# Down's weight folds spread over places, one fetch moved ahead of the transposing loads, and the fold steps of gate and up shifted

## The chip, the cores and the metric

The kernel runs on one core of one Trainium2 chip. A core has five engines with a queue each, which run in order and wait for each other only through semaphores: TensorE (PE in the profile, its weight loads are PEld), VectorE (DVE), ScalarE (ACT), GpSimd (POOL) and SyncE (SP). SP computes nothing; it issues the transfers between DRAM and the on-chip memories, which 16 DMA engines then carry out. TensorE writes its results to PSUM, a small memory that VectorE and ScalarE read. The metric is the device time of one execution in microseconds; before the change the median of three runs was 1569.95 us (1569.58 to 1570.46).

## The reference

The input x is (8, 512, 512) in float32: 8 sequences of 512 tokens and 512 channels. Cut to what matters:

```python
xn = layernorm(x)                                   # over channels
q, k, v = xn @ Wq.T + bq, xn @ Wk.T + bk, xn @ Wv.T + bv
kv = cumsum((elu(k) + 1) * v, axis=tokens)          # linear attention, elementwise per channel
s = ((elu(q) + 1) * kv * 32**-0.5) @ Wo.T + bo
h = fwht(xn * SU_ug) / 64                           # normalized Hadamard transform over 512
u = (h @ W_up.T) * (Wscale_ug[:2048] * 64)
g = (h @ W_gate.T) * (Wscale_ug[2048:] * 64)
d = fwht(silu(g) * u * SU_dp) / 64                  # over 2048
d = (d @ W_down.T) * (Wscale_dp * 64)
out = x + s * silu(d)
```

## The kernel before

**Products.** Every matrix product is done with seven products instead of eight for each 2 x 2 split of its operands. Both operands carry seven factors, at the indices P1 to P7: four are given, the other three (and a changed P7) are sums and differences of them ("encode"). The seven products are summed in PSUM and by VectorE. The helper group (L442) does it for q, k, v, gate and up with 512 tokens in the columns; token_groups (L512) for o and down, with tokens in the rows; hidden_unit with block_product (L622, L803) does it on two levels at once for gate and up together ("gu"). TensorE works in float32.

**Pairs.** The outer loop takes the eight sequences in four pairs p. A pair runs k, v, q twice (attention), then four units u of gate, up and their gated product "ho", with o after the first unit and half of down after the second and the fourth. In the first pair the weights have to be made first: gate and up in units 0 to 2 come from raw weights, one matrix block at a time, and only unit 3 and all units of the later pairs take ready two-level weights ("gu", streamed from d_gu).

**Folded weights.** The Hadamard transforms and the signs are moved into the weights. For one block of gate or up, folded_w (L919) loads the raw block and returns three steps with a number of places each: butterflies (four VectorE additions), fold (two TensorE products with the 128 x 128 Hadamard matrix `had`, evicted by four ScalarE activations, L945) and encode (four VectorE operations, L305 to L308). For a block f of 4 or more, encode also queues inner_w, which forms the two-level factors (L408) and stores them to d_gu.

**Down's weights** are made during the first pair. begin_down (L1144) and chain_down (L1149) take the matrix in four blocks o of 128 columns, 1 MB each: load_down (L960) loads block o into the working tile rd; butterflies_down (L963) queues ten VectorE operations of 128 x 1024 (two scales, L974, and four levels of two, L969); fold_down (L983) issues four TensorE products with `had`, each evicted by four ScalarE activations (L994), and stores the block to wd_f in DRAM. Once all four are there, first_half_down (L999) loads what the first half of down needs, forms its factors and stores them to d_down 0; the second half is made in four parts by down_w (L374), queued behind groups 16 to 19. wd_made counts the stored parts of each half; a half is ready at 4.

**Places.** The order of the work around these is written by hand. `at(n, fn)` (L422) enters a step n places ahead in an agenda; advance runs the agenda. A group takes 14 places, and a place is half of the time of a product over two blocks (two 128 x 512 matmuls each). VectorE work that is not urgent goes into a list with later() and is popped by pace() (L89) behind an output on VectorE, up to a given time of work (1.7 us by default in group); `urgent` goes ahead of `idle`. catch_up (L96) pops all of it. block_product doesn't pace.

**Weights ahead.** `queue` (L1067) holds all weights in the order of their use, ask(n) (L1082) requests them so that n are ahead (three), and get_w takes one. The steps of a requested block are entered at `e["place"] = max(now + steps[k][0], place + 4)` (L1105): the butterflies of the block two ahead, the fold and the encode of the next one. For a weight of down, stream_w (L323) first makes sure that its half is ready: it pops the lists until wd_made is 4 (L330 to L333).

**The hand-over to the next pair.** After the last unit, next_tokens (L238) loads the normalized tokens of the next pair transposed ("z", eight loads of 256 KB from d_x, squares, L225) and queues VectorE's transposes. Then the first half's result of down, d, is fetched back from DRAM (fetch, L748, two of 1 MB), later s and y, and down's second half begins. z of the odd sequence, d, s, y and the tiles a, v, u, r of a unit share six buffers, t8; the streamed weights share four, wpool.

**From program order to queues.** The framework plans the queue of each engine from the traced program with its own costs: an instruction can be issued ahead of one that was traced before it if its inputs and its buffer are ready sooner by those costs. keep_in_program_order (L938, L987) holds a fold behind what was traced before it on TensorE, issue_after holds paced work behind its output, and background (L75) lowers the priority of what it traces.

Of the kernel before, what the change touches and what calls it, by code (L numbers as in the profile page):

```python
# [8 lines left out]
F32 = mybir.dt.float32  # L9
# [12 lines left out]
def kernel(  # L22
# [66 lines left out]
    def pace(ins, us):  # L89
        while us > 0 and (urgent or idle):  # L90
            t, fn, args = (urgent or idle).pop(0)
            with tc.issue_after(ins.ins):
                fn(*args)
            us -= t
# [228 lines left out]
    def stream_w(name):  # L323
        w = new_w("%s_%s" % (name[0], name[1] if type(name[1]) is int else "%d_%d" % name[1]))
        if name[0] == "gu":
            u, i = name[1]
            nc.sync.dma_start(w, inner[u][:, i])
        elif name[0] == "down":
            h, i = name[1]
            while wd_made[h] < 4:  # L330
                assert urgent or idle
                _, fn, args = (urgent or idle).pop(0)
                fn(*args)  # L333
            w = by_factor(w, 4)
            nc.sync.dma_start(w, wd[h][:, i])
        else:
            nc.sync.dma_start(flat(w), kept["%s_%d" % name])
            if name[0] == "o":
                w = by_factor(w)
        return w  # L340
# [98 lines left out]
        return ps.tile([P, n, L // n], F32, tag=tag, bufs={"px": 3, "py": 1, "pz": 2, "t": 2}[tag], name=f"{tag}_{name}")  # L439


    def group(name, ws, rhs, dst, then, bias=(None, None)):  # L442

        n = len(ws)
        u = n

        def product(p, i, first):
            for k in range(n):  # L450
                r = rhs(k, i)
                nc.tensor.matmul(  # L452
                    p.rearrange("p a t -> p (a t)") if len(r.shape) == 2 else p, ws[k][:, i, :], r,
                    start=(first and k == 0), stop=(k == n - 1), skip_group_check=True,
                )

        def snapshot(what, i):
            s = snap.tile([P, L], F32, tag="s", name=f"{what}_{name}")
            b = bias[min(i, 1)]
            p = px.rearrange("p a t -> p (a t)")  # L460
            if b is None:
                nc.scalar.copy(s, p)
            else:
                nc.scalar.activation(s, p, AF.Identity, bias=b)
            return s

        def output(i, s, p):
            pace(nc.vector.tensor_tensor(dst[i], s, p.rearrange("p a t -> p (a t)"), ALU.add), 1.7)  # L468

        px, py, pz = (bank(t, name, 2) for t in ("px", "py", "pz"))  # L470
        sums = {}

        def p1():
            product(px, P1, True)
            sums["a"] = snapshot("sa", 0)

        def p2():
            product(py, P2, True)
            output(0, sums["a"], py)

        def p6():
            product(px, P6, False)
            sums["b"] = snapshot("sb", 1)

        def p7():
            product(pz, P7, True)

        def p5():
            product(px, P5, False)
            sums["c"] = snapshot("sc", 2)  # L490
            output(2, sums["c"], pz)

        def p3():
            product(px, P3, False)

        def p4():
            product(pz, P4, False)
            output(1, sums["b"], pz)
            then(px.rearrange("p a t -> p (a t)"))

        at(0, p1)
        at(u, p2)
        at(3 * u, p6)
        at(5 * u, p7)
        at(6 * u, p5)
        at(9 * u, p3)
        at(11 * u, p4)
        advance(7 * u)
        between()
# [174 lines left out]
    def attention(p, xo, co, get_w):  # L684
        def project(m, g, then):
            w = get_w(m, g)
            r = t8.tile([P, 2, 2, L], F32, tag="t", name=f"{m}_{p}_{g}")
            b = (col("b" + m, g), col("b" + m, g + 2))

            def whole(px):  # L690
                nc.scalar.activation(r[:, 0, 1], px, AF.Identity, bias=b[0])  # L691
                then(r)

            group(
                f"{m}_{p}_{g}", [w[:, 0], w[:, 1]], x_rhs(xo),
                (r[:, 0, 0], r[:, 1, 0], r[:, 1, 1]), whole, b,
            )

        def elu_plus_one(r, name):
            neg = t8.tile([P, 2, 2, L], F32, tag="t", name=f"neg_{name}")  # L700
            for h in range(2):
                nc.scalar.activation(neg[:, h], r[:, h], AF.Relu, scale=-1.0)
                nc.scalar.activation(neg[:, h], neg[:, h], AF.Exp, scale=-1.0)
                nc.vector.scalar_tensor_tensor(r[:, h], r[:, h], 1.0, neg[:, h], ALU.add, ALU.max)

        def heads(g):
            phi = {}

            def with_k(k):
                phi["k"] = k  # L710
                elu_plus_one(k, f"k_{p}_{g}")

            def with_v(v):
                k = phi["k"]
                for h in range(2):
                    nc.gpsimd.tensor_tensor(v[:, h], v[:, h], k[:, h], ALU.mult)  # L716
                at(4, lambda: sums(k, v))

            def sums(k, v):
                for h in range(2):  # L720
                    for s in range(2):
                        nc.vector.tensor_tensor_scan(  # L722
                            k[:, h, s], ones.to_broadcast([P, L]), v[:, h, s], 0.0, ALU.mult, ALU.add
                        )

            def with_q(q):
                k = phi["k"]
                elu_plus_one(q, f"q_{p}_{g}")
                for h in range(2):
                    nc.vector.scalar_tensor_tensor(  # L730
                        co[:, g, h : h + 3 : 2, :], k[:, h], QSCALE, q[:, h], ALU.mult, ALU.mult
                    )
                encode_tokens(nc.gpsimd, co[:, g])

            project("k", g, with_k)
            project("v", g, with_v)
            project("q", g, with_q)

        for g in range(2):
            heads(g)  # L740
# [178 lines left out]
    def folded_w(name, src, f, room=None):  # L919
# [32 lines left out]
                with background():  # L952
                    inner_w(name, f - NU, folded[name, f - NU], w)

        return w, [(6, butterflies), (5, fold), (9, encode)]

    folded = {}
    wd_f = dram.tile([FF, D], F32, tag="wd_f", name="wd_f")

    def load_down(o):  # L960
        nc.sync.dma_start(rs[:, o % 2], wdown_t[:, o * P : (o + 1) * P].rearrange("(c p) e -> p c e", p=P))

    def butterflies_down(o, then):  # L963
# [16 lines left out]
                later(1.2, half, i, dst, src, h)  # L980
        later(0.0, then)

    def fold_down(o):  # L983
        r = rs[:, o % 2]
        for a in range(NF // 4):
            p = ps.tile([P, 4, P], F32, tag="t", name=f"pwd_{o}_{a}")
            tc.keep_in_program_order(  # L987
                nc.tensor.matmul(
                    p.rearrange("p c e -> p (c e)"), had,
                    r[:, 4 * a : 4 * a + 4].rearrange("p c e -> p (c e)"), start=True, stop=True,  # L990
                )
            )
            for c in range(4):
                nc.scalar.activation(  # L994
                    r[:, 4 * a + c], p[:, c], AF.Copy, scale=su_dp[:, 4 * a + c : 4 * a + c + 1]
                )
        nc.sync.dma_start(wd_f[:, o * P : (o + 1) * P].rearrange("(c p) e -> p c e", p=P), r)

    def first_half_down():  # L999

# [80 lines left out]

    def ask(n):  # L1082
        while queue and len(ahead) < n:
            p, m, g = queue.pop(0)
            w, steps = (first_w if p == 0 and m not in ("down", "gu") else later_w)(m, g)
            ahead.append({"key": (m, g), "w": w, "steps": steps, "traced": 0, "asked": 0, "place": 0})

# [56 lines left out]
    def begin_down():  # L1144
        nc.sync.dma_start(wsc_r, wscale_dp.partition_broadcast(P))
        load_down(0)
        at(12, lambda: chain_down(0))

    def chain_down(o):  # L1149
        def folded_block():  # L1150
            fold_down(o)
            if o + 2 < KD:
                at(8, lambda: load_down(o + 2))
            if o + 1 == KD:
                at(8, first_half_down)

        def then():
            at(10, folded_block)
            if o + 1 < KD:
                at(4, lambda: chain_down(o + 1))  # L1160

        butterflies_down(o, then)
# [14 lines left out]
    for p in range(B // 2):  # L1177
# [11 lines left out]
        for u in range(NU):  # L1189
# [23 lines left out]
            if u == 1:  # L1213
                if p == 0:
                    weights_ahead(NU - 1)
                down(p, 0, hos, get_w)
                if p == 0:
                    inner_tokens(xo)
                hos = []
        if more:  # L1220
            catch_up()
            next_tokens(2 * p + 2, xo)
        ds = [fetch(f"d_{p}_{s}") for s in range(2)]
        ss, ys = [], []
        at(7, lambda: ss.extend([fetch(f"s_{p}_{s}") for s in range(2)]))
        at(15, lambda: ys.extend([load_y(p, s) for s in range(2)]))
# [52 lines left out]
```

## Time and profile before

| | us |
|---|---|
| median of three runs | 1569.95 |
| profiled execution | 1564.62 |
| its span | 1562.80 |
| TensorE busy | 1529.4 |
| VectorE busy | 985.1 |
| GpSimd busy | 497.5 |
| ScalarE busy | 418.8 |

The profile shows one execution. "Busy" counts the time in which an engine computes; a queue that only waits or issues transfers is not busy. A wait is told as the engine and its line, the engine and line that released it, and the sum, number and longest of such waits; a timeline line as start, length, engine, line, operation, output <- inputs, shapes and number, with the idle time before it in brackets. A name such as px_gate is the PSUM tile px of the product gate, pw and pwd are the PSUM tiles of the folds of gate or up and of down, w_down is a weight tile of down and d_down the DRAM tensor it comes from.

### The profile page before, as it was taken

How to read it: one execution, taken by the hardware profiler on the slowest of the kernel's cores; microseconds unless marked ns; L12 is line 12 of the kernel's file. 1: busy time of each engine (PE TensorE's matmuls, PEld its weight loads, DVE VectorE, ACT ScalarE, POOL GpSimd, SP SyncE). 2: the span in 40 equal slices, each digit the busy share in tenths (PEclk: the TensorE clock that was granted, in tenths of full speed). 3: DMA queues.
4: the chain of work that ended last, by engine and by line, in shares of the span. 5: the costliest groups of instructions: out<-in, count | busy, mean ns of one | idle time of the engine just before them, and what ended most of it. 6: DMA issues, size and time to landing. Idle time of an engine off the chain costs nothing.

```text
span 1562.8 us, 15732 instructions
## 1 busy us (share of the span) xinstructions
PE 1529.4 (98%) x5924; PEld 1127.0 (72%) x5924; DVE 985.1 (63%) x1379; ACT 418.8 (27%) x664; POOL 497.5 (32%) x280
## 2 busy tenths in 40 slices
PE   7999999998999999999999999999999999999998
PEld 3335545845884588888885488888886468888887
DVE  5897785677866674716676574725675476543673
ACT  4443341142114521112215431111212431111211
POOL 4633144004321262304612235301622236110731
PEclk9999999999999999999999999999999999999999
DMA  8244867797785344344575434336474233535462
GB/s 280 78 153 152 268 218 225 232 275 270 200 304 196 91 158 155 108 152 165 157 286 213 102 137 148 135 102 195 153 249 171 85 106 117 185 99 177 155 260 85
DMA packets 197693, 273.31 MB, mean 175 GB/s; under 512 B 56817, under 2 KB 155121, under 8 KB 193393
## 3 DMA queue, kind: packets, MB, share of 16 engines
q1 hardware_dynamic: 197472, 272.27, 53.3%
q8 instruction: 47, 0.77, 0.2%
q14 instruction: 30, 0.24, 0.0%
q10 hardware_dynamic: 144, 0.03, 0.0%
HBM read 196.25 MB, written 76.02 MB: 174 GB/s over the span
## 4 chain that ended last, share of the span: by engine, by line
PE 88%; DVE 4%; DMA 3%; issue 2%; POOL 1%; ACT 1%; SPq 1%; POOLq 0%; DVEq 0%; ACTq 0%
PE px_gu L630 20%; PE px_dn L528 13%; PE pz_gu L630 10%; PE pz_dn L528 6%; PE py_gu L630 5%; PE py_dn L528 4%; PE px_k L452 3%; PE px_v L452 3%; PE px_o L528 3%; PE px_q L452 3%; PE pz_o L528 2%; PE pz_k L452 2%; PE px_gate L452 2%; PE pz_q L452 2%; PE pz_v L452 1%
## 5 line engine op out<-in xcount | busy, mean ns | idle before, releaser
L630 PE MATMUL px_gu<-xo,w_gu 128*128 128x256 f32 x1456 | 348.9, 381 | 0.0
L630 PEld LDWEIGHTS px_gu<-xo,w_gu 128*128 128x128 f32 x1456 | 277.5, 191 | 44.2 <-issue 5.0
L528 PE MATMUL px_dn<-w_down,ho 128*128 128x256 f32 x1024 | 228.9, 379 | 0.0
L528 PEld LDWEIGHTS px_dn<-w_down,ho 128*128 128x128 f32 x1024 | 194.9, 190 | 28.7 <-issue 2.9
L630 PE MATMUL pz_gu<-xo,w_gu 128*128 128x256 f32 x728 | 188.6, 382 | 5.4 <-DVE a L661 5.2
L831 POOL TENSOR_TENSOR u<-u,v 128x1024 f32<-128x1024 f32 x26 | 60.8, 2363 | 371.2 <-DVE u L668 347.5
L630 PEld LDWEIGHTS pz_gu<-xo,w_gu 128*128 128x128 f32 x728 | 138.3, 191 | 26.2 <-DVE a L661 6.1
L528 PE MATMUL pz_dn<-w_down,ho 128*128 128x256 f32 x496 | 112.4, 380 | 3.2 <-DVE u L468 3.2
L528 PEld LDWEIGHTS pz_dn<-w_down,ho 128*128 128x128 f32 x496 | 93.9, 190 | 17.0 <-DVE u L468 3.6
L630 PE MATMUL py_gu<-xo,w_gu 128*128 128x256 f32 x364 | 93.5, 379 | 0.0
L876 POOL TENSOR_TENSOR s<-s,d 128x512 f32<-128x512 f32 x30 | 40.0, 1333 | 165.5 <-ACT d L875 126.4
L716 POOL TENSOR_TENSOR v<-v,k 128x1024 f32<-128x1024 f32 x16 | 43.0, 2685 | 138.9 <-ACT v L691 111.2
L630 PEld LDWEIGHTS py_gu<-xo,w_gu 128*128 128x128 f32 x364 | 69.3, 190 | 9.3
L835 POOL TENSOR_TENSOR v<-v,r 128x1024 f32<-128x1024 f32 x26 | 60.9, 2362 | 27.7 <-DVE r L668 27.7
L793 POOL TENSOR_TENSOR ho<-g,u 128x512 f32<-128x512 f32 x6 | 10.9, 1812 | 161.0 <-DVE u L468 151.1
L452 PE MATMUL px_k<-xo,w_k 128*128 128x512 f32 x128 | 61.6, 603 | 0.0
L452 PE MATMUL px_v<-xo,w_v 128*128 128x512 f32 x128 | 60.8, 595 | 0.0
L821 ACT ACTIVATE a<-a,cols_sb 128x512 f32<-128x512 f32 x26 | 18.8, 722 | 155.2 <-DVE a L668 153.4
L452 PE MATMUL px_q<-xo,w_q 128*128 128x512 f32 x128 | 60.2, 593 | 0.0
L722 DVE TENSOR_TENSOR_SCAN k<-ones,v 128x512 f32<-128x512 f32 x32 | 40.9, 1317 | 28.6 <-POOL v L716 28.6
L528 PE MATMUL px_o<-w_o,co 128*128 128x256 f32 x256 | 58.4, 380 | 0.0
L875 ACT ACTIVATE d<-d 128x512 f32<-128x512 f32 x31 | 19.5, 630 | 144.5 <-DVE d L543 102.4
(264 smaller groups left out, 2476.5 us busy)
## 6 DMA issues: line engine op xcount, KB each, us to landing
w_gu<-d_gu SPq DMA_DIRECT2D x91, 896.0 KB, 4.4
w_down<-d_down SPq DMA_DIRECT2D x56, 512.0 KB, 3.6
d_s<-o SPq DMA_DIRECT2D x8, 1024.0 KB, 4.3
d_d<-dn SPq DMA_DIRECT2D x8, 1024.0 KB, 7.7
d<-d_d SPq DMA_DIRECT2D x8, 1024.0 KB, 6.2
s<-d_s SPq DMA_DIRECT2D x8, 1024.0 KB, 8.1
y<-in_x_dram SPq DMA_DIRECT2D x8, 1024.0 KB, 7.3
out_dram<-y SPq DMA_DIRECT2D x15, 512.0 KB, 3.3
```

The costliest lines, as they stand in the source:

```text
L452: nc.tensor.matmul(p.rearrange("p a t -> p (a t)") if len(r.shape) == 2 else p, ws[k][:, i, :], r, start=(first and k == 0), stop=(k == n ...
L528: nc.tensor.matmul(p[:, c], t[:, (2 * g + c) * P : (2 * g + c + 1) * P], ws[i](k), start=(first and k == 0 and c == cs[0]), stop=(k == n - ...
L630: nc.tensor.matmul(p[:, lane], w[:, lane, i, :], x[:, i, :], start=(first and lane == 0), stop=True, skip_group_check=True,)
L716: nc.gpsimd.tensor_tensor(v[:, h], v[:, h], k[:, h], ALU.mult)
L722: nc.vector.tensor_tensor_scan(k[:, h, s], ones.to_broadcast([P, L]), v[:, h, s], 0.0, ALU.mult, ALU.add)
L793: nc.gpsimd.tensor_tensor(ho[:, P1], g[:, 0, 0], r[:, 0, 0], ALU.mult)
L821: nc.scalar.activation(g[:, m], g[:, m], AF.Silu, scale=col("w_gate", u + m * NU + a * NG))
L831: nc.gpsimd.tensor_tensor(r[:, m], ru1[:, m], rv[:, m], ALU.add)
L835: nc.gpsimd.tensor_tensor(rv[:, m], rv[:, m], rr[:, m], ALU.add)
L875: nc.scalar.activation(d, d, AF.Silu)
L876: (nc.vector if final and (a, s) == (1, 0) else nc.gpsimd).tensor_tensor(r, r, d, ALU.mult)
```

## The change

Five edits, all of order. (1) fold_down does one of a block's four folds and enters the next one two places later; the store to wd_f follows the last. (2) chain_down for a block starts only when its load was issued 14 places ago ("loaded"), and looks again every two places; before, block 0 started 12 places after its load and the others four places after the block ahead. (3) ask no longer forces a half of down to be ready: while it isn't and other weights are still ahead, it stops asking; only when none is ahead does it run the agenda and the lists until the half is there. stream_w only asserts it. (4) The butterflies of gate and up are entered 5 places ahead instead of 6, their fold 7 instead of 5. (5) d is fetched before catch_up and next_tokens instead of behind them. The argument `time` of group keeps its value of 1.7.

```diff
@@ stream_w
             h, i = name[1]
-            while wd_made[h] < 4:
-                assert urgent or idle
-                _, fn, args = (urgent or idle).pop(0)
-                fn(*args)
+            assert wd_made[h] == 4
             w = by_factor(w, 4)
@@ folded_w
-        return w, [(6, butterflies), (5, fold), (9, encode)]
+        return w, [(5, butterflies), (7, fold), (9, encode)]
@@ load_down, fold_down
+    loaded = []
+
     def load_down(o):
+        at(14, lambda: loaded.append(o))
         nc.sync.dma_start(rs[:, o % 2], wdown_t[:, o * P : (o + 1) * P].rearrange("(c p) e -> p c e", p=P))
...
-    def fold_down(o):
+    def fold_down(o, a, then):
+
         r = rs[:, o % 2]
-        for a in range(NF // 4):
-            p = ps.tile([P, 4, P], F32, tag="t", name=f"pwd_{o}_{a}")
-            tc.keep_in_program_order(
-                nc.tensor.matmul(
-                    p.rearrange("p c e -> p (c e)"), had,
-                    r[:, 4 * a : 4 * a + 4].rearrange("p c e -> p (c e)"), start=True, stop=True,
-                )
+        p = ps.tile([P, 4, P], F32, tag="t", name=f"pwd_{o}_{a}")
+        tc.keep_in_program_order(
+            nc.tensor.matmul(
+                p.rearrange("p c e -> p (c e)"), had,
+                r[:, 4 * a : 4 * a + 4].rearrange("p c e -> p (c e)"), start=True, stop=True,
             )
-            for c in range(4):
-                nc.scalar.activation(
-                    r[:, 4 * a + c], p[:, c], AF.Copy, scale=su_dp[:, 4 * a + c : 4 * a + c + 1]
-                )
+        )
+        for c in range(4):
+            nc.scalar.activation(
+                r[:, 4 * a + c], p[:, c], AF.Copy, scale=su_dp[:, 4 * a + c : 4 * a + c + 1]
+            )
+        if a + 1 < NF // 4:
+            at(2, lambda: fold_down(o, a + 1, then))
+            return
         nc.sync.dma_start(wd_f[:, o * P : (o + 1) * P].rearrange("(c p) e -> p c e", p=P), r)
+        then()
@@ ask
         while queue and len(ahead) < n:
-            p, m, g = queue.pop(0)
+            p, m, g = queue[0]
+            if m == "down" and wd_made[g[0]] < 4:
+                if ahead:
+                    break
+                while wd_made[g[0]] < 4:
+                    if not urgent and not idle:
+                        advance(1)
+                    catch_up()
+            queue.pop(0)
@@ begin_down, chain_down
         load_down(0)
-        at(12, lambda: chain_down(0))
+        chain_down(0)
 
     def chain_down(o):
+        if o not in loaded:
+            at(2, lambda: chain_down(o))
+            return
+
         def folded_block():
-            fold_down(o)
             if o + 2 < KD:
                 at(8, lambda: load_down(o + 2))
             if o + 1 == KD:
                 at(8, first_half_down)
 
         def then():
-            at(10, folded_block)
+            at(10, lambda: fold_down(o, 0, folded_block))
             if o + 1 < KD:
                 at(4, lambda: chain_down(o + 1))
@@ the loop over pairs
+        ds = [fetch(f"d_{p}_{s}") for s in range(2)]
         if more:
             catch_up()
             next_tokens(2 * p + 2, xo)
-        ds = [fetch(f"d_{p}_{s}") for s in range(2)]
```

More of the change, by code (lines that the diff above doesn't have):

```diff
@@ L439, in bank, with group @@
         return ps.tile([P, n, L // n], F32, tag=tag, bufs={"px": 3, "py": 1, "pz": 2, "t": 2}[tag], name=f"{tag}_{name}")
-    def group(name, ws, rhs, dst, then, bias=(None, None)):
+    def group(name, ws, rhs, dst, then, bias=(None, None), time=1.7):
         n = len(ws)
@@ L467, in output @@
         def output(i, s, p):
-            pace(nc.vector.tensor_tensor(dst[i], s, p.rearrange("p a t -> p (a t)"), ALU.add), 1.7)
+            pace(nc.vector.tensor_tensor(dst[i], s, p.rearrange("p a t -> p (a t)"), ALU.add), time)
         px, py, pz = (bank(t, name, 2) for t in ("px", "py", "pz"))
@@ L695, in project @@
                 f"{m}_{p}_{g}", [w[:, 0], w[:, 1]], x_rhs(xo),
[L696 removed]
+                (r[:, 0, 0], r[:, 1, 0], r[:, 1, 1]), whole, b, 1.7,
             )
```

## The prediction

> **What bounds the kernel now.** I read the page's first part, then TensorE's waits, the busy times of short stretches, and the timelines of the queues where a wait stands. The page and the summary of waits, for TensorE:
>
> ```profile
> span 1562.8 us, 15732 instructions
> PE 1529.4 (98%) x5924; PEld 1127.0 (72%) x5924; DVE 985.1 (63%) x1379; ACT 418.8 (27%) x664; POOL 497.5 (32%) x280
> ...
> PE pz_gu L630 <- DVE a L661: 5.2, 1, 5.2
> PE pz_q L452 <- DVE q L468: 3.4, 1, 3.4
> PE pz_dn L528 <- DVE u L468: 3.2, 1, 3.2
> PE pwd L988 <- ACT w_gate L945: 3.2, 1, 3.2
> PE pz_o L528 <- DVE g L468: 2.9, 1, 2.9
> PE px_gate L452 <- ACT sc_gate L462: 0.9, 1, 0.9
> ```
>
> TensorE is the bound: 33.4 us of the span are idle, 8.2 before its work starts (7.4 and 0.8 in the same view), 5.7 in the last pair, and the six waits above, 18.8 us, all in the first pair, before 384 us. No other engine or queue costs anything except by making TensorE wait. So the change can win at most these waits and the slow matmuls behind them. The columns of the next lines are stretch, its length, busy us of PE, PEld, DVE, ACT, POOL, granted clock, DMA share, GB/s:
>
> ```profile
> 100.00:120.00 20.00, 16.85 (x32) 6.74 (x31) 19.38 (x19) 12.39 (x27) 10.43 (x7) 0.83 0.44 142
> 380.00:400.00 20.00, 16.92 (x68) 14.54 (x69) 17.77 (x34) 3.94 (x5) 2.99 (x3) 0.83 0.63 227
> 400.00:420.00 20.00, 20.00 (x94) 17.65 (x93) 15.37 (x23) 4.33 (x6) 12.91 (x6) 1.00 0.83 199
> ```
>
> After a wait the granted clock falls to 0.83. Behind the 5.16 us wait at 378, 4 matmuls took 2.07 us (a full-clock group of 4 takes 1.03) and 8 took 3.33 (1.89): 2.5 us lost; behind the 3.21 us at 263, nothing.
>
> The stretch 400 to 420 has no wait at all. It is where the first pair goes over to the second half of down, and the place that decides the forecast. SP's timeline there, then the same place in the second pair, where z comes from tokens stored long before:
>
> ```profile
> 403.00 0.65 SPq L235 DMA_DIRECT2D z<-d_x  x1
> 404.71 6.36 SPq L335 DMA_DIRECT2D w_down<-d_down  x2
> 411.12 11.20 SPq L235 DMA_DIRECT2D z<-d_x  x7
> 422.43 2.48 SPq L750 DMA_DIRECT2D d<-d_d  x2
> 425.00 1.06 SPq L335 DMA_DIRECT2D w_down<-d_down  x2
> ...
> 762.45 1.19 SPq L235 DMA_DIRECT2D z<-d_x  x1
> 768.12 0.33 SPq L335 DMA_DIRECT2D w_down<-d_down  x1
> 768.50 0.57 SPq L235 DMA_DIRECT2D z<-d_x  x1
> 774.16 0.32 SPq L335 DMA_DIRECT2D w_down<-d_down  x1
> 774.53 3.02 SPq L235 DMA_DIRECT2D z<-d_x  x2
> ```
>
> The first two w_down are traced before z, the third after z and d. The first two overtake z as soon as a weight buffer is free; the third, whose buffer comes free about 6 us after the second's (the spacing 404.71, 410.76), is issued only at 425.00, behind all of z and d. So the planner takes, among what it holds ready, what was traced first, and it books several us of SP for one z: between the ready times of two w_down it fits one z and no second one. Then the lines that meet it, on TensorE, POOL and VectorE:
>
> ```profile
> 416.60 2.75 PE L528 MATMUL px_dn<-w_down,ho 128*128 128x256 f32 x12
> 419.19 1.03 PE L630 MATMUL px_gu<-xo,w_gu 128*128 128x256 f32 x4
> ...
> 424.54 1.13 PE L630 MATMUL pz_gu<-xo,w_gu 128*128 128x256 f32 x4
> ...
> 416.24 2.37 POOL L822 TENSOR_TENSOR ho<-v 128x1024 f32<-128x1024 f32 x1 [0.83 <-ACT v L821]
> ...
> 379.58 2.85 DVE L333 TENSOR_TENSOR wd<-wd 128x256 f32<-128x256 f32 x3 [4.57 <-DMA wd<-wd_f]
> ```
>
> The first w_down is used at 416.60. L333 is the loop in stream_w that pops the last down_w encoding: its presence shows that wd_made[1] was below 4 when the second half's first weight was asked for.
>
> **The change, part by part.** Nothing is added or taken away on any engine: 16 fold matmuls, 64 evictions, 40 butterfly and scale operations and the same transfers. All is order. Sums are made against the profiled execution: span 1562.80, 1.82 around it, 1564.62 in all, which is 5.33 below the median of 1569.95.
>
> *The ask.* Two weights of down's second half (P1 and P7) were asked for at the get of the sixth and seventh gu product, places 397 and 404 (14 places to a group, a place 0.86 us: two products of 1.72 us take four). Now ask stops while wd_made is below 4. Between the last down_w's encode (place 370) and the end of the unit (411) nothing pops the list, since block_product doesn't pace; catch_up at 411 does. Both asks are held, and P1, P7 and P2 are asked together inside down, traced after d and all eight z. By the rule just read they stand where the third w_down stood. SP then: d0 takes the t8 buffer that z took, long free; z0 at 403.0; d1 waits for the buffer of a (POOL's L822 at 406.24, 2.36 us: 408.6); the other three of the first z, 0.6 each; the second z waits for the buffer of v, which POOL's L822 frees at 416.24+2.37 = 418.6; four z, 0.6 each, then w_down at about 421.2. Landing: a w_down took 3.6 us on the median, 5.6 behind two z and two d (782.45 to 788.08), 7.6 behind seven and two (425.00 to 432.57); I take 6.0, nearest to the second, so 427.2. TensorE: what it still has of gu ends at about 425.4, set by VectorE's reads, not by down. Until then it did 28 down matmuls before (12+12+4, at 0.216 us 6.05 us), so the same work started at 427.2 is late by 427.2 - (425.4 - 6.05) = 7.9 us. Bounds: 0, if w_down is issued ahead of the second z (at about 411, landing 414.5 before 416.6); 13.2, if it lands at 432.57 as the third did. Slow clock behind it: 0 to 2.5 by the two rows; the idle time is in pieces, so I take 2.0. After it the second and third weights are there and all down steps shift alike; the next pair's tokens depend on z and d, which get no later than 422 + 6. Part: **+9.9 us**, 0 to +15.7.
>
> [...]
>
> *d ahead of z.* Three times two 1 MB fetches move past eight z on SP. In pairs 2 and 3 the ask is as before, d gets the buffer z had, z the one d1 had (782.03): its four issues end near 784.5, so the third w_down goes out 2 us later than 782.45 and lands near 790 for a use at 796.6; z lands near 790 for a transpose at 800.7. Covered: 0. If the cover failed, 2 us a pair.
>
> *Folds and down's chain.* chain_down(0) queues at place 28 and not 26, so block 0's five VectorE pairs move one pacing slot (26, 30, 36, 40, 44 to 30, 36, 40, 44, 50). Block 1's stay. Block 2 must wait for its load, issued 10 places later: its pairs go from 86, 92, 106, 110, 112 to 106, 110, 112, 114, 120. Folds: 60, 92, 124, 138 become 64-70, 92-98, 130-136, 144-150; the first half's loads 146 to 158, its store 174 to 184, still before the ask at 196, so that one isn't held.
> The wait at 56 (3.4): a pair (L969, 4.50 us beside POOL; 2.35 alone) still stands ahead of q's output: 0, or -0.7 because POOL's encoding at 39.8 meets one pair less.
> The wait at 106 (3.2): the first fold of block 1 waits for the eviction of gate's fold, which stands on ACT behind a Silu that waits for VectorE's g at 106.86. Spreading the folds leaves the first one there. With gate's fold two places later, q's L691, L702 and a copy L462 (0.70, 1.06, 0.57) are ready ahead of the eviction: up to +2.3; if it were gone, -3.2 and 3.0 of slow clock.
> The waits at 135 and 143 (0.9 and 2.9) absorb that: their end, 145.8, is set by VectorE. There a fourth pair (+2.35) now stands before g's output; against it the wait of L408 for d_gu<-s_gate (7.2 us to land behind the 1 MB wd_f store, now six places later; median 3.5) ends some 2 us sooner, and the 0.9 goes. Net **+0.7**; bounds -5.6 (both waits and 1.8 of slow clock gone) and +3.4 (the pair and 1 us for a missing cover).
> The first half's factors (two pairs) move to 170 and 176 beside gate's outputs: VectorE had 3.3 us idle at 216 for it; 0 to +1 for the chain to the 3.2 us wait at 263. The 5.2 us wait at 378 stays: VectorE takes the down_w encodings as soon as it deems them loaded, wherever they were traced.
>
> *Butterflies at 5, fold at 7.* The encode follows at max(9, 7+4) = 11. Four operations of 0.68 us a weight; a fold needs 1.7 on TensorE and 1.7 on ACT, and has seven places (6 us) until the first product. weights_ahead keeps its own places. 0, but for ACT's order above.
>
> Sum: 9.9 + 0.7 = **+10.6**: 1575.2 for the profiled execution, **1580.6** for the median.
>
> **Rivals.**
> *The late ask is hidden:* the planner books less for a z, and w_down goes ahead of the second z; SP reaches it by 411 and it lands before 416.6. For it: three of four t8 buffers come late. Against: the third w_down's place before. Then the first pair's waits alone decide: 1569.95 + 0.7 = 1570.7, from 1566.8 to 1573.
> *Faster:* the late ask is hidden, and the folds' wait goes with that at 143: -5.6, 1564.4. For it: the eviction stands only two places from the fold. Against: ACT's Silu.
> *Slower by VectorE alone:* ask hidden, up's butterflies (2.7 us) and the fourth pair both ahead of g's output at 145: +2.35+2.7 less 1.7 = +3.4, 1573.4. It decides once w_up lands before 120's pacing.
>
> **How the numbers follow.** Late ask seen by TensorE: 0.63 (1575 to 1586, by the bounds 0 to 13.2, without its lowest third). Hidden, within 0.2%: 0.20. Hidden and faster: 0.11. Hidden and slower: 0.06. 0.2% is 3.1 us, about what a measurement can tell. Faster 0.11, same 0.20, slower 0.69. The range 1567 to 1586 leaves out most of the faster case and the top of the late one.
>
> **What would show it.** Right: SP has z and d ahead of the first w_down, issued after 418, and PE px_dn waits for w_down's DMA near 420, with a clock under 1.00 behind. Wrong: w_down near 405 to 411 and no such wait; pwd's wait at 106 gone; or the wait at 378 gone too, which would win 7.7 back.

## The result, and the profile after

The changed kernel takes 1579.05 us in the median of four runs (1576.41 to 1581.25); the kernel before took 1569.76 beside it (1565.57 to 1570.46). The ratio is 1.0072, with a 95% interval of 1.0057 to 1.0087: slower, by 9.3 us between the medians, against 10.6 us forecast. (The two medians alone stand at 1.0059; a ratio of 1.0072 is 11.3 us.) The profiled execution took 1576.41 us, with a span of 1574.6, 11.8 more than the span shown for before.

The page's first lines and the summary of TensorE's waits, of the changed kernel (waiting operation and line, releaser and line, us in all, times, longest):

```profile
span 1574.6 us, 15723 instructions
PE 1530.5 (97%) x5924; PEld 1124.0 (71%) x5924; DVE 996.9 (63%) x1379; ACT 418.6 (27%) x663; POOL 495.8 (31%) x280
...
PE px_dn L525 <- DMA w_down<-d_down: 8.0, 1, 8.0
...
PE pwd L988 <- ACT rd L994: 3.9, 2, 3.4
...
PE pz_gu L627 <- DVE a L658: 2.2, 1, 2.2
PE pz_dn L525 <- DVE u L465: 1.8, 1, 1.8
PE pw_gate L936 <- DVE r_gate L930: 1.8, 1, 1.8
PE px_k L449 <- ACT sa_k L461: 1.7, 1, 1.7
```

TensorE computes for as long as before (1530.5 against 1529.4 us); what was added is idle time. The first line of the waits is new and by far the longest that the change made. Three more are new: a fold of down that waits for an eviction (3.9), a fold of gate (1.8) and a product of k (1.7). Two of before have shrunk, pz_gu's from 5.2 to 2.2 and pz_dn's from 3.2 to 1.8, and that of pz_o is as good as gone. The prediction had only the first of all these.

SP's timeline of the changed kernel at the hand-over (start, length, line, operation, number of issues), and behind it TensorE's:

```profile
398.68 0.50 SPq L747 DMA_DIRECT2D d<-d_d  x1
403.15 0.65 SPq L235 DMA_DIRECT2D z<-d_x  x1
405.76 0.32 SPq L747 DMA_DIRECT2D d<-d_d  x1
406.12 14.76 SPq L235 DMA_DIRECT2D z<-d_x  x7
420.98 2.65 SPq L332 DMA_DIRECT2D w_down<-d_down  x4
```

```profile
417.46 1.13 PE L627 MATMUL pz_gu<-xo,w_gu 128*128 128x256 f32 x4 [0.78 <-DVE u L658]
426.60 7.94 PE L525 MATMUL px_dn<-w_down,ho 128*128 128x256 f32 x24 [8.00 <-DMA w_down<-d_down]
434.38 5.34 PE L525 MATMUL pz_dn<-w_down,ho 128*128 128x256 f32 x24
```

The first w_down of the second half stands behind both d and all eight z and is issued at 420.98. TensorE, which before began on it at 416.60, begins at 426.60. Until then it has only gu's last products, for which VectorE is too slow (0.78 us idle here and 0.79 two us earlier), then nothing for 8.00 us; and the 24 matmuls behind the wait take 7.94 us where the next 24 take 5.34.

### The profile page after: what moved, and what is told of

The parts are those of the page before. It is cut to its first block, busy times and chain, and to the rows that moved or that the text cites. A ratio compares the mean times of both kernels' runs of the same rounds, so it can differ in the third digit from the quotient of the medians.

```text
span 1574.6 us, 15723 instructions
## 1 busy us (share of the span) xinstructions
PE 1530.5 (97%) x5924; PEld 1124.0 (71%) x5924; DVE 996.9 (63%) x1379; ACT 418.6 (27%) x663; POOL 495.8 (31%) x280
## 4 chain that ended last, share of the span: by engine, by line
PE 81%; DVE 10%; DMA 4%; issue 2%; POOL 1%; SPq 1%; ACT 1%; POOLq 0%; DVEq 0%; ACTq 0%
PE px_gu L627 19%; PE px_dn L525 12%; PE pz_gu L627 10%; PE pz_dn L525 6%; PE py_gu L627 5%; PE py_dn L525 3%; PE px_o L525 3%; PE px_k L449 3%; PE px_v L449 3%; PE px_q L449 3%; PE pz_o L525 2%; PE px_gate L449 2%; DVE rd L969 1%; PE pz_k L449 1%; PE pz_v L449 1%
## 5 line engine op out<-in xcount | busy, mean ns | idle before, releaser
L525 PEld LDWEIGHTS pz_dn<-w_down,ho 128*128 128x128 f32 x496 | 93.7, 190 | 15.8 <-DVE u L465 2.2
L525 PE MATMUL py_dn<-w_down,ho 128*128 128x256 f32 x256 | 57.9, 379 | 0.0
```

The lines of the kernel that those rows point to most:

```text
L525: nc.tensor.matmul(p[:, c], t[:, (2 * g + c) * P : (2 * g + c + 1) * P], ws[i](k), start=(first and k == 0 and c == cs[0]), stop=(k == n - ...
```

## The experiments

Each run stands beside runs of the kernel before on the same chip; their median there lay between 1565.6 and 1567.6 us, so the ratios are compared, not the times. In the diffs, "-" is the kernel named as the base.

### Is it the late ask?

Base: the changed kernel; the ask forces the half to be ready, as before.

```diff
@@ ask
-            p, m, g = queue[0]
-            if m == "down" and wd_made[g[0]] < 4:
...
-            queue.pop(0)
+            p, m, g = queue.pop(0)
+            while m == "down" and wd_made[g[0]] < 4:
+                _, fn, args = (urgent or idle).pop(0)
+                fn(*args)
```

> The changed kernel, except that the ask for a weight of down's second half encodes what is still on the list, as before, and does not stop. Theory (the late ask is nearly the whole loss): w_down is issued before z's third to seventh fetch, TensorE's 8.0 us wait for it near 420 and the 2.6 us of slow matmuls behind it go, the other waits stay as they are in the changed kernel (3.4 us near 83, 2.2 near 381): 1567 to 1571 us, ratio to before 0.998 to 1.001. Rival (the spread folds and their new wait near 83 are the loss): at least 1575, since they are all still there. Rival (d fetched ahead of z is the loss, by taking buffers and queue time from w_down): 1576 to 1580, with the wait near 420 still there.

Measured: 1563.54 us against 1567.63, ratio 0.9975 (0.9964 to 0.9986). So the rest of the change doesn't merely cost nothing, as forecast: it makes the kernel faster, and the held ask costs 1.0072/0.9975, or 1.0%, some 15 us; the two profiled spans are 12.9 us apart (1574.6 and 1561.7). TensorE's waits of this run near the places at issue:

```profile
PE pwd L988 <- ACT rd L994: 3.8, 2, 3.4
...
PE py_dn L525 <- DMA w_down<-d_down: 0.3, 1, 0.3
```

Of w_down's wait 0.3 us are left; the new wait of the folds (3.8) is still there, and so are the shrunken ones (2.2 for pz_gu, 1.7 for pz_dn). The rival that blamed the folds for the loss falls, and so does the one that blamed d.

The same edit the other way round: the kernel before, with the changed kernel's ask and nothing else.

> The kernel before with the held ask alone: folds, butterflies and the order of d and z as before. Theory: the three w_down are issued together behind z's seven fetches, at 418 to 423 us, TensorE waits 6 to 9 us for the first of them and 2 to 3 us more go in a slow clock: 1578 to 1582 us, ratio 1.005 to 1.008. Rival (folds or d ahead of z): 1569 to 1571, ratio 0.999 to 1.001, no wait at 420.

Measured: 1578.8 us against 1567.63, ratio 1.0072 (1.0052 to 1.0092). The held ask alone loses as much as the whole change. SP's and TensorE's timelines of this run:

```profile
418.62 4.30 SPq L750 DMA_DIRECT2D d<-d_d  x2
423.01 2.77 SPq L335 DMA_DIRECT2D w_down<-d_down  x4
```

```profile
429.02 7.11 PE L528 MATMUL px_dn<-w_down,ho 128*128 128x256 f32 x24 [3.60 <-DMA w_down<-d_down]
```

All eight z are issued from 406.96 on, then d; w_down is last here too. The wait itself is shorter than expected (3.60 against 6 to 9), because gu ended later in this run, at 425.4 us against 418.6 in the changed kernel, and w_down was issued only 2 us later. Around it come two pieces of 0.8 us ahead, 1.8 us of slow matmuls behind (7.11 us for 24, where 5.34 is usual) and waits of 1.5 and 1.0 us for px_k near 484 and 494; together 9.4 us, where the same places of the changed kernel give 13.9.

### d ahead of z

The kernel before, with d's fetches ahead of catch_up and next_tokens.

```diff
+        ds = [fetch(f"d_{p}_{s}") for s in range(2)]
         if more:
             catch_up()
             next_tokens(2 * p + 2, xo)
-        ds = [fetch(f"d_{p}_{s}") for s in range(2)]
```

> The kernel before with d's two fetches ahead of z alone, in all three pairs. Theory: covered by the lead that z and w_down have: 1569 to 1571 us, ratio 0.999 to 1.001, no wait of TensorE for a w_down. Rival (d's 1 MB fetches push w_down back): a wait for w_down in the first pair near 420 and up to 2 us in each of the two later pairs: 1573 to 1580.

Measured: 1567.45 us against 1567.63, ratio 1.0 (0.999 to 1.0009); no wait for a w_down. This edit costs nothing.

### Does the order behind z cost, or the later encoding?

Base: the changed kernel with its hold. At the first pair's hand-over the list is emptied and down's weights are asked for ahead of d and z, three of them in the first run, two in the second.

```diff
+        if p == 0:
+            catch_up()
+            ask(3)          # second run: ask(2)
         ds = [fetch(f"d_{p}_{s}") for s in range(2)]
```

> The changed kernel, ask held as it is, but at the hand-over of the first pair the list is emptied and down's three weights are asked for ahead of d and z. Theory (what costs is the place in trace order behind z, not the later encoding): w_down is issued at 400 to 412 us, TensorE's 8.0 us wait near 420 and its slow clock go: 1562 to 1566 us, as without the hold, ratio 0.996 to 0.999. Rival (the hold itself makes it late: encode, store and fetch start 8 to 14 places later): a wait of over 4 us for w_down stays, 1570 to 1577.

Measured: 1572.95 us against 1565.61, ratio 1.0048 (1.0033 to 1.0063). That is the rival's time, and a wait of over 4 us for a w_down is there as it said, but not the one it meant. The wait near 420 is gone (the first w_down is issued at 401.81, its products begin at 413.7), but there is another one 33 us later. SP's timeline, then TensorE's:

```profile
428.45 17.84 SPq L906 DMA_DIRECT2D y<-in_x_dram  x2
446.34 1.62 SPq L332 DMA_DIRECT2D w_down<-d_down  x3
```

```profile
452.89 7.36 PE L525 MATMUL px_dn<-w_down,ho 128*128 128x256 f32 x19 [7.49 <-DMA w_down<-d_down]
```

The second y stood on SP from 428.9 to 445.9, and the next three w_down behind it. Whether that is the hold's own doing or that of the third early weight, the second run tells:

> As the run that asked for three weights ahead of d and z, but for two of them; the third is asked for inside down, as in the kernel before. Theory (the held ask costs by its place behind z alone; the 7.5 us wait near 453 came from the trace order that a third early ask made, with the fifth w_down behind a y that had no buffer): neither the wait near 420 nor that near 453, ratio 0.996 to 0.999. Rival (the second wait is the hold's own, weights being later through it): a wait of over 4 us for a w_down between 440 and 460, ratio over 1.003.

Measured: 1563.16 us against 1567.38, ratio 0.9972 (0.9961 to 0.9983). SP's timeline of this run:

```profile
401.89 0.32 SPq L332 DMA_DIRECT2D w_down<-d_down  x1
...
407.94 0.32 SPq L332 DMA_DIRECT2D w_down<-d_down  x1
408.30 17.70 SPq L235 DMA_DIRECT2D z<-d_x  x8
...
428.88 0.61 SPq L906 DMA_DIRECT2D y<-in_x_dram  x1
429.58 1.37 SPq L332 DMA_DIRECT2D w_down<-d_down  x2
```

The ask is still held until the hand-over; its place in the program order differs from the changed kernel's, and the loss is gone. Compared operation by operation, the queues of all five engines in this trace are those of the run without the hold: from the earlier place the planner makes the same queues as if nothing had been held. Nor was the encoding later in the changed kernel: VectorE's operations stand there in the order of the run without the hold up to 414 us, and the last part of down's second half is stored at 383.8 us (384.8 without the hold, 384.0 before). So the place behind d and z is what costs. One weight more asked ahead was enough to let the second y overtake the w_down that it here lets pass.

### Which part gains, and which pays for the folds?

The change without the hold is at 0.9975, where the prediction had +0.7 us. Its parts, each alone on the kernel before. First the folds: spread by two places, with the chain tied to the loads (edits 1 and 2 of the change).

> The kernel before with down's folds spread two places apart and its chain tied to the loads, and nothing else. Theory: the new wait of block 0's folds near 83 us (3.4 to 3.9 us) is paid, the wait of g's output at 145 (2.9) goes in return: 1568 to 1572 us, ratio 0.999 to 1.0015. Rival (the spread folds are the loss): 1574 to 1579, ratio over 1.003.

Measured: 1570.81 us against 1567.63, ratio 1.0022 (1.0012 to 1.0031). By the ratio that lies between the two expectations: a loss of 3.2 us. Then edit 2 without edit 1, the four folds of a block again at one place:

```diff
@@ load_down, begin_down, chain_down
+        at(14, lambda: loaded.append(o))
...
-        at(12, lambda: chain_down(0))
+        chain_down(0)
...
+        if o not in loaded:
+            at(2, lambda: chain_down(o))
+            return
```

> The kernel before with down's chain tied to the loads alone; the four folds of a block stay at one place. Theory (the 3.2 us that the folds alone lost come from the spread, through the wait of block 0's third fold near 82 for an eviction): no such wait, 1566 to 1569 us, ratio 0.999 to 1.001. Rival (the later chain costs, by VectorE's work near 120 to 145): 1570 to 1573, ratio over 1.001, with longer waits between 115 and 155.

Measured: 1570.53 us against 1565.61, ratio 1.0027 (1.0013 to 1.0041). The rival was right: the loss is there without the spread. But its longest new wait is near 82, not between 115 and 155, where the rival had it. TensorE's waits for evictions of down's folds, of the folds alone and then of the chain alone:

```profile
PE pwd L991 <- ACT rd L997: 7.0, 3, 3.4
```

```profile
PE pwd L991 <- ACT rd L997: 7.9, 2, 5.1
```

Near 82 us block 0's folds wait 5.1 us when they are together and 3.4 and 0.85 when spread. ScalarE's timeline of the changed kernel shows why; three evictions of the first fold are over by 76.1, then come:

```profile
81.58 1.06 ACT L699 ACTIVATE neg_k<-k 128x1024 f32<-128x1024 f32 x1 [5.43 <-DVE k L465]
82.54 0.35 ACT L994 ACTIVATE rd<-pwd,su_dp 128x128 f32<-128x128 f32 x1
```

The fourth eviction of the first fold stands on ScalarE behind the Relu of k (L699), which waits for k's output on VectorE; that stands behind four butterflies of gate, up to 80.9. The folds share two PSUM buffers, so the third fold waits for that one small eviction. In the kernel before all sixteen evictions of block 0 (72.5 to 77.6) were done ahead of this Relu, which began at 80.95.

Base of the next two: the changed kernel without the hold (0.9975). In the first, block 0's folds are at one place and the other blocks' spread; in the second, block 0 counts as loaded 12 places behind its load and not 14.

```diff
@@ fold_down (first run)
         if a + 1 < NF // 4:
-            at(2, lambda: fold_down(o, a + 1, then))
+            if o == 0:
+                fold_down(o, a + 1, then)
+            else:
+                at(2, lambda: fold_down(o, a + 1, then))
             return
@@ load_down (second run)
-        at(14, lambda: loaded.append(o))
+        at(12 if o == 0 else 14, lambda: loaded.append(o))
```

> The changed kernel without the hold (1563.5), and with the four folds of block 0 at one place again; blocks 1 to 3 stay spread. Theory (the waits of block 0's third and fourth fold, 3.4 and 0.4, and slow matmuls behind them, are paid in full): 1557 to 1561 us, ratio 0.993 to 0.996. Rival (VectorE sets what follows, so the time comes back as waits near 106 to 145): 1562 to 1565, ratio 0.997 to 0.999.

Measured: 1566.05 us against 1565.61, ratio 1.0009 (1.0 to 1.0019): neither. Taking the spread of block 0 away loses the whole gain; the wait near 82 grows to 5.1 (from 3.4 and 0.3), and that of the next block's fold from 3.4 to 3.9. Spreading softens what the later chain brought. These two make 1.9 us of some 5; behind them the queues differ in many places (px_gate has a new wait of 1.7 near 137), and the rest is not accounted for.

> The changed kernel without the hold (ratio 0.9975), and with block 0 deemed loaded 12 places behind its load and not 14, so that its chain begins at place 26 as in the kernel before; folds spread. Theory (the later chain makes the waits of block 0's folds near 83, 5.1 us with the folds together and 3.8 spread, and these come back only in part): no wait over 1 us near 83, ratio 0.993 to 0.9965. Rival (VectorE's work sets the end of the first 170 us anyway): that wait goes and others between 100 and 155 grow by as much, ratio 0.9965 to 0.999.

Measured: 1561.63 us against 1567.38, ratio 0.9967 (0.9954 to 0.998), not apart from 0.9975. The wait stayed (3.4 and 0.85 near 83), but the edit had moved nothing: operation by operation, the queues of all five engines are those of the run without the hold. VectorE begins block 0 behind q's output in both (at 41.18 us here and 41.43 there), where the kernel before has it ahead of that output (38.70). So the wait's price, and whether block 0's later start alone makes it, stay open. This run and the one with two weights asked first are repeats of the run without the hold: 0.9975, 0.9972 and 0.9967 are one order, measured three times.

Last, edit 4, the places of gate's and up's steps: both numbers, then each alone.

```diff
-        return w, [(6, butterflies), (5, fold), (9, encode)]
+        return w, [(5, butterflies), (7, fold), (9, encode)]   # first run
+        return w, [(5, butterflies), (5, fold), (9, encode)]   # second run
+        return w, [(6, butterflies), (7, fold), (9, encode)]   # third run
```

> The kernel before with gate's and up's butterflies at place 5 and their fold at 7 and nothing else. Theory (the 7 us between the folds alone, 1570.8, and the change without the hold, 1563.5, is these places' doing, by the order of VectorE's work near 145 and near 380): the waits at 135 and 143 (0.9 and 2.9) or that at 378 (5.2) shrink also here: 1561 to 1565 us, ratio 0.996 to 0.998. Rival (the gain needs the spread folds as well): those waits stay, 1566 to 1569, ratio 0.999 to 1.001.

Measured: 1561.85 us against 1565.61, ratio 0.9977 (0.9968 to 0.9987). The gain doesn't need the folds.

> The kernel before with gate's and up's butterflies at 5 and the fold left at 5 (encode at 9). Theory (the gain of the two places together, ratio 0.9977, is the butterflies': they stand elsewhere among VectorE's work, so that the waits at 263 and 378 are broken into shorter ones): 0.996 to 0.9985, the 5.2 us wait near 380 under 4. Rival (the fold's two places): 0.999 to 1.001, the 5.2 us wait as before.

Measured: 1566.96 us against 1567.38, ratio 0.9998 (0.9989 to 1.0008). The theory falls: the butterflies' place does nothing, and the queues of this run are those of the kernel before, operation by operation.

> The kernel before with gate's and up's fold at 7 and the butterflies left at 6 (encode at 11). Theory (the gain is the butterflies'): 0.999 to 1.001, the 5.2 us wait near 380 as before. Rival (the fold's two places are the gain, by ACT's and TensorE's order): 0.996 to 0.9985, that wait under 4 us.

Measured: 1560.97 us against 1567.38, ratio 0.9957 (0.9942 to 0.9972). The fold's two places are the gain. Here too the butterflies' place left no trace: operation by operation, the queues of this run are those of the run with both numbers, so that 0.9977 and 0.9957 are two measurements of one order, on two chips. This one number, changed in the kernel before, beats both kernels by that; it isn't apart from the change without the hold (0.9967 to 0.9975).

Two waits answer to it in every kernel that was run (us, of the summaries of waits):

| kernel | fold at | wait of pz_dn near 265 | pw_gate near 272 | wait of pz_gu near 380 |
|---|---|---|---|---|
| before | 5 | 3.2 | none | 5.2 |
| held ask alone | 5 | 3.8 | none | 5.2 |
| d first alone | 5 | 4.2 | none | 5.2 |
| folds alone | 5 | 3.5 | none | 5.2 |
| chain alone | 5 | 4.3 | none | 5.2 |
| butterflies at 5 | 5 | 4.6 | none | 5.2 |
| fold at 7 | 7 | 0.8 | 1.8 | 2.2 |
| both places | 7 | 1.4 | 1.8 | 1.0 |
| changed kernel | 7 | 1.8 | 1.8 | 2.2 |
| without the hold | 7 | 1.7 | 1.8 | 2.2 |
| block 0 together | 7 | 2.4 | none | 2.2 |
| block 0 sooner | 7 | 1.4 | 1.8 | 2.2 |
| two asked first | 7 | 0.8 | 1.8 | 2.2 |

The rows before, held ask alone, d first alone and butterflies at 5 have one order up to 403 us, and so do fold at 7 and both places: how far they differ (3.2 to 4.6 near 265, 1.0 to 2.2 near 380) is the scatter of single executions, and the step from 5 to 7 is clear of it. ("Both places" has a wait of 3.2 for up's pz at 375.7 besides; the run with three asked first, also at 7, has 0.4, 1.8 and 2.2.) VectorE's timeline near 263, of the kernel before and then of the fold at 7, shows what changed places:

```profile
264.31 0.68 DVE L931 TENSOR_TENSOR r_gate<-w_gate 128x512 f32<-128x512 f32 x1
265.02 0.69 DVE L932 TENSOR_TENSOR r_gate<-r_gate 128x512 f32<-128x512 f32 x1
265.63 0.68 DVE L468 TENSOR_TENSOR u<-sb_up,pz_up 128x512 f32<-128x512 f32 x1
```

```profile
262.61 0.68 DVE L468 TENSOR_TENSOR u<-sb_up,pz_up 128x512 f32<-128x512 f32 x1
263.20 0.69 DVE L930 TENSOR_TENSOR r_gate<-w_gate 128x512 f32<-128x512 f32 x1
```

Before, u's output, for whose PSUM buffer TensorE waits, stood behind three butterflies of the next weight; with the fold later it stands ahead of them, and what is late instead is the fold, by 1.8 us. Near 380 it is the same with the encoding of down_w, which waits for its load. VectorE's timeline of the fold at 7:

```profile
377.62 0.63 DVE L333 TENSOR_TENSOR wd<-wd 128x256 f32<-128x256 f32 x1 [3.83 <-DMA wd<-wd_f]
378.18 0.68 DVE L661 TENSOR_TENSOR a<-sc_gu,pz_gu 128x512 f32<-128x512 f32 x1
...
379.37 2.18 DVE L333 TENSOR_TENSOR wd<-wd 128x256 f32<-128x256 f32 x3
```

Of the late encoding one operation and not three now stands ahead of a's output. The first half of down begins at 250.3 us in this run (250.9 before) and the second at 412.2 (416.6), so most of the gain lies between, where these two waits are. That the order changed is shown; why the planner, for a fold two places later, books VectorE's work elsewhere is not settled.

## Why the prediction was right or wrong

The time, the sign and the cause were right, but the sum came out as closely as it did because two errors of opposite sign met in it, the ask's too small and the rest's too large; that much was luck.

**The ask: right in mechanism, too small in size.** Each link is in the trace of after: d and all eight z ahead, w_down issued at 420.98 (421.2 forecast), first products at 426.60 (427.2), a wait of 8.00 us (7.9) and slow matmuls behind it, 2.6 us (2.0). The two runs on the ask give 0.7% to 1.0%, 11 to 15 us, where the step had 9.9. The step had 7.9 us for all of the idle time; measured were 9.6, the 8.00 and the two pieces of 0.8 ahead of it. Those come in where gu's last products wait for VectorE; in the run with two weights asked first, as before, down's products stand there. In the changed kernel the next pair has a wait of 1.7 us at 482.8 (px_k for an eviction on ScalarE) as well, which the run without the hold doesn't have (the run with the held ask alone has two, 1.5 and 1.0); the step said that everything behind would shift alike. The rule drawn from the order on SP, that among what is ready the first traced is issued first and that z counts for several us, agrees with the run with two weights asked ahead, whose third w_down is issued at 426.09, behind all eight z.

**d ahead of z: right.** Forecast 0, measured 1.0 (0.999 to 1.0009).

**Folds and chain: right only at the end of its bounds.** Forecast +0.7 (-5.6 to +3.4), measured +3.2 for the two edits alone. The step that failed is "block 0's five VectorE pairs move one pacing slot ... 0, or -0.7": it looked at VectorE's order alone. The wait at 56 shrank in the folds alone (3.4 to 2.3), but not surely by the change: it lies between 1.9 and 3.5 in the eight traces in which block 0 starts behind q's output, and at 3.3 to 3.4 in the other six. The folds, moved on by the same slot, put an eviction behind k's Relu on ScalarE, and there are the waits near 82. The waits at 135 and 143, which were to absorb such things, stayed in that run (2.1 and 3.0).

**Butterflies and fold: wrong.** The step "0, but for ACT's order" measured -6.4 us for the fold's place alone (ratio 0.9957) and -3.8 for both numbers (0.9977), which are two measurements of the same queues. It counted the time a fold needs and the places it has, and found that there was room. It should have asked what the move does to the order on the neighbours' queue: the gain is VectorE's output going ahead of work that is needed later.

**"The 5.2 us wait at 378 stays": wrong.** It fell to 2.2 or less wherever the fold is at 7 (with both places alone, up's wait of 3.2 at 375.7 took its place in part). The reason given, that VectorE takes the encodings as soon as it deems them loaded, holds; but how many of them stand ahead of a's output was taken as fixed. The prediction named this as a sign that the result would be better, yet by another cause.

**The rivals.** That w_down is hidden, and that a new wait on VectorE alone makes the loss, both fall with the run with the held ask alone. The faster case (0.11) had about the right size for the rest of the change (0.9975 without the hold), and the wait at 143 that it built on did go (2.9 to 0.2 us in the changed kernel); but new waits near 83 (3.9 us) stood against it, and the gains near 265 and 380 through the fold's place were not thought of.

## What to carry to other kernels

When a request is held back, look less at when it becomes possible than at what has been traced ahead of it by then: here the same hold cost 0.7 to 1.0% with the requests behind eight loads and nothing with two of them ahead; with three ahead it cost again, by a load that stood for 17 us on SP ahead of the next weights. Move a step by its own need and you have looked at one engine only: ask which outputs of the neighbouring engines change places with it, above all those whose PSUM buffer the bottleneck waits for. Run the parts of a change alone: one number of this one, the fold's 7, gives 0.9957 to 0.9977 where the whole gives 1.0072. And compare the queues before explaining a difference: four of the runs here turned out to be repeats of another.

## What the runs showed of the hardware

The clock behind a wait is not set by the length of the wait alone. TensorE's timeline behind the fold of down near 109, first of the kernel before, then of the run with d first alone:

```profile
109.05 3.78 PE L988 MATMUL pwd<-rd,had 128*128 128x512 f32 x4 [3.15 <-ACT w_gate L945]
```

```profile
108.76 1.98 PE L988 MATMUL pwd<-rd,had 128*128 128x512 f32 x4 [3.16 <-ACT w_gate L945]
```

The same wait, 3.15 and 3.16 us, and the same four matmuls: 3.78 us in one and 1.98 in the other, at a granted clock of 0.66 and 0.98 between 108 and 118. Nor is a shorter wait safe. After the wait of 2.20 us near 380, the next eight took 3.16 us in the fold at 7 and 1.89 in the changed kernel without the hold:

```profile
378.90 1.13 PE L630 MATMUL pz_gu<-xo,w_gu 128*128 128x256 f32 x4 [2.20 <-DVE a L661]
379.87 3.16 PE L630 MATMUL px_gu<-xo,w_gu 128*128 128x256 f32 x8
```

```profile
382.07 1.13 PE L627 MATMUL pz_gu<-xo,w_gu 128*128 128x256 f32 x4 [2.20 <-DVE a L658]
383.04 1.89 PE L627 MATMUL px_gu<-xo,w_gu 128*128 128x256 f32 x8
```

The granted clock of the two kernels' traces shows more. While TensorE works, each has four stretches at a clock of 0.50: from 60.17, 107.95, 145.50 and 381.02 us in the kernel before, 3.41, 6.83, 3.41 and 6.83 us long, and from 59.66, 83.55, 114.27 and 421.47 in the changed kernel, 3.41, 3.41, 6.83 and 10.24 long. So each is 3.41 us long, or two or three times that, and within a trace the starts lie whole multiples of 3.41 us apart: 14, 25 and 94 behind the first one before, 7, 16 and 106 after. Below, a window is one such step of 3.41 us, laid through these starts. The windows around the 2.20 us wait, in the fold at 7 and then in the changed kernel without the hold, each laid by its own trace (columns as in the prediction: behind the stretch and its length stands TensorE's busy time, and the clock is the number ahead of the last two):

```profile
376.92:380.33 3.41, 1.43 (x7) 1.27 (x8) 2.71 (x4) 0.46 (x1) 3.41 (x3) 1.00 0.89 317
380.33:383.75 3.42, 3.42 (x10) 2.70 (x9) 3.13 (x7) 0.59 (x1) 0.27 (x1) 0.50 1.06 413
```

```profile
377.98:381.40 3.42, 1.89 (x9) 1.33 (x7) 0.82 (x2) 1.17 (x2) 3.34 (x3) 1.00 1.01 333
381.40:384.81 3.41, 2.74 (x13) 2.43 (x14) 3.41 (x7) 0.00 (x0) 2.37 (x2) 1.00 1.08 428
384.81:388.22 3.41, 2.64 (x13) 2.00 (x12) 3.41 (x8) 0.58 (x1) 0.00 (x0) 1.00 0.97 385
```

In the first the wait lies nearly whole in one window, which is idle for 1.98 of its 3.41 us, and the next one is slow, though the wait is over by then. In the second it is split over two windows, idle for 1.53 and 0.67, and the clock stays. Counted over the traces of the two kernels, from their first clock record (15.8 and 15.3 us) to the end of TensorE's work: of the windows at full clock, each of the eight with 2.05 us or more of idle time is followed by a slow one, none of the 883 with 1.82 or less. Of the slow windows, the five with 1.10 us or more of idle time are followed by another slow one, the eight with 0.47 or less by a fast one. These are counts from two traces, in which the ends of matmuls are modelled, not a rule beyond them.

What such a stretch costs can be read from the matmuls: behind the 3.15 us wait near 109 3.0 us (1.9 in the four matmuls shown and 1.1 in the next four, 2.96 us where 1.88 is usual), behind the 8.00 us wait for w_down 2.6 (7.94 us for 24, against 5.34). An estimate from the granted clock of 0.50, half of the time for which TensorE works in the stretch, comes near: 2.9 us of 5.73 and 2.6 of 5.12; over the eight stretches of the two traces it gives 1.5 to 2.9 us each. The prediction's case without a loss, the 3.21 us at 263, was a wait that its execution split 1.82 and 1.39 between two windows, both at a clock of 1.00; in the run with d first alone, of the same order there, the wait of 4.20 us is followed by twelve matmuls in 5.48 us instead of 2.86. The prediction took its 0 for the slow clock from that case, in one execution.
